# ScalarE's instructions in the program's own order, exponentials and scores in fixed turns of buffers

## The chip, the cores and the metric

The kernel runs on one core of a Trainium2 chip. The metric is the device time of one execution in microseconds, the median of three runs. A profiled execution of the same program gives the trace.

## What is computed

Input x has four images of 128 channels and 64 x 64 positions. Per image (batch):

- a group norm, a convolution that yields offsets and a mask, a deformable 3 x 3 convolution (bilinear samples gathered at shifted positions, weighted with the mask), added to x;
- each position is now a token of 128 values. A layer norm; cosines of the values plus an angle and running products of these give features for 16 heads of 8 values; attention over all 4096 tokens of the image with these features as queries, keys and values alike; an output matrix, layer norm, a small feed-forward of 512 with a relu, layer norm, added to the tokens;
- a layer norm, a router over 8 experts with softmax, the two best, and the weighted sum of their 128 x 128 products, added.

```
qkv = _qz_ring(heads + rx_theta)
scores = einsum('bhsd,bhtd->bhst', q, q) / sqrt(D)
ctx = einsum('bhst,bhtd->bhsd', softmax(scores), q)
```

Since queries and keys are the same features, the matrix of exponentials is symmetric: a tile of it, transposed, serves another pair of chunks.

## The kernel before

**Attention steps.** Tokens are cut into 8 chunks of 512, keys into 32 tiles of 128, heads into 4 groups of 4. A *run* is one (batch, group, chunk of queries); a *step* (run, t) handles key tile t of a run. There are 3700 steps, written out by a loop over n that issues the scores of step n+2 (LAG = 2) ahead of the context of step n. Per step:

- `scores` (L1250): four matmuls, one a head, into two PSUM tiles `sc` of 128 x 1024 (tag "sc", three buffers);
- two exponentials on ScalarE (L1259), from `sc` to two SBUF tiles `e` of 128 x 1024 (tag "e", six buffers);
- `context` (L1267): four matmuls (each recorded twice), which read `e` and add to the accumulator `acc`. At a run's end VectorE moves `acc` to `cu` (L1471, L1473).

In order of PE's queue: scores of step t, filler, context of step t-2, scores of step t+1.

**Tiles given away.** Four steps of most runs are in `gives`. For these `turn` (L1141) lets VectorE transpose both `e` tiles in 32 x 32 blocks into a tile `st` (three buffers), which SyncE stores to DRAM (`etd`). The next run loads them (`et`, two buffers) and uses them in `from_turned` (L1203), which saves it four steps' scores and exponentials. So an `e` tile of such a step has two readers, TensorE and VectorE.

**Work beside it.** `Beside` holds generators: `prepare` (group norm, the table of the image in DRAM, offsets, gathers by POOL at L625, weighting on VectorE at L645 to L651, transposes, convolution, features) for the next batch, `finish` (output matrix, feed-forward, experts) for chunks whose four groups are done, up to two chunks at a time, and `turned`. Each generator yields what it next needs of PE and VectorE (`need`), and the loop puts it among the steps by a plan of its own with 1.82 us a step. `beside.later(when, emit)` emits an instruction when the plan's clock reaches `when`; `beside.dve` is when the plan has VectorE done.

**Who orders.** The block of the main loop is under `tc.manual_schedule(engines={PE, DVE, SP, POOL})`: for these four engines the order of the program is kept. ScalarE isn't named, so the framework's scheduler places its instructions, and gives out the buffers of pools with more than one by its own idea of when each comes free. Besides the exponentials ScalarE runs 8 `mk` (L559, the mask's exponential), 32 `ex` (L1017, the router's softmax), and the DMA issues of the constants (`fill`, L293; those with late=True are emitted after the first table) and of six of the table's stores (L501).

The lines that the change moves:

```
        mk = temp("mk", KK, half)
        nc.scalar.activation(mk, om[:, :, 18:27], AF.Exp, scale=-1.0)
...
        nc.scalar.activation(ex, lg, AF.Exp)
```

Of the kernel before, what the change touches and what calls it, by code (L numbers as in the profile page):

```python
# [9 lines left out]
F32 = mybir.dt.float32  # L10
I32 = mybir.dt.int32
F32R = mybir.dt.float32r
AF = mybir.ActivationFunctionType
ALU = mybir.AluOpType
AX = mybir.AxisListType
PE = mybir.EngineType.PE
DVE = mybir.EngineType.DVE
SP = mybir.EngineType.SP
POOL = mybir.EngineType.Pool
PSUM = bass.MemoryType.PSUM  # L20
DRAM = bass.MemoryType.DRAM

P = 128
# [176 lines left out]
def need(pe=0.0, dve=0.0, lat=0.0, hold=False, after=0.0):  # L200

    return pe, dve, lat, hold, after


def ve(n, ops=1):

    return ops * (0.17 + n / 960.0)
# [6 lines left out]
def tr(n):  # L216

    return 0.13 + 0.115 * n
# [3 lines left out]
def kernel(  # L222
# [22 lines left out]
    nc = tc.nc  # L245
# [5 lines left out]
    big = ctx.enter_context(tc.tile_pool(name="big", bufs=1))  # L251
    work = ctx.enter_context(tc.tile_pool(name="work", bufs=2))
    dram = ctx.enter_context(tc.tile_pool(name="table", bufs=1, space=DRAM))
    ps_s = ctx.enter_context(tc.tile_pool(name="ps_s", bufs=3, space=PSUM))
    ps_a = ctx.enter_context(tc.tile_pool(name="ps_a", bufs=1, space=PSUM))
    ps_m = ctx.enter_context(tc.tile_pool(name="ps_m", bufs=1, space=PSUM))

    beside = Beside()
# [2 lines left out]

    progress = {}
    featuring = []

    summed = []


    alone = []

    def misc(name):  # L270
        if alone:
            return ps_s.tile([P, 2, 512], F32, tag="sc", name=name)[:, 0, :]
        return ps_m.tile([P, 512], F32, tag="misc", name=name)

    def by_columns(dst, lhsT, rhs, start, stop):
# [139 lines left out]
    for i in range(NFX):  # L415
        t = big.tile([P, 4, QR], F32, name=f"fx{i}")
# [91 lines left out]
    def offsets(b, xn, idx, wt, rest):  # L508


        xn3 = xn.rearrange("p (h w) -> p h w", w=WW)
        HB = NBLK // 2

        def temp(name, n, half):
            return work.tile([P, HB, n], F32, tag="p2", name=f"{name}{b}_{half}", bufs=NP2)

        def products(half, got):

            for n, k in enumerate((4, 0, 1, 2, 3, 5, 6, 7, 8)):
                for top in range(0, 8, 4):
                    last = n == KK - 1 and top == 4
                    yield need(pe=MM256, dve=ve(512) if last else 0.0, lat=0.2 if last else FREE, hold=not last)
                    if n == 0 and top == 0:
                        po = misc(f"om_ps{b}_{half}")
                        p3 = po.rearrange("p (h w) -> p h w", w=WW)
                    dy, dx = k // 3 - 1, k % 3 - 1
                    for c in range(4):
                        r0 = 32 * half + 8 * c  # L530
                        ra, rb_ = max(r0 + top, -dy), min(r0 + top + 4, HH - dy)
                        ca, cb = max(0, -dx), min(WW, WW - dx)
                        nc.tensor.matmul(  # L533
                            p3[32 * c : 32 * (c + 1), ra - r0 : rb_ - r0, ca:cb],
                            lhsT=wom_sb[:, k, :],
                            rhs=xn3[:, ra + dy : rb_ + dy, ca + dx : cb + dx],
                            start=(n == 0 and top == 0), stop=last,
                        )
            oc = work.tile([P, 512], F32, tag="p2", name=f"oc{b}_{half}", bufs=NP2)
            nc.vector.tensor_scalar(oc, po, bom_sb, None, ALU.add)  # L540
            yield need(pe=tr(4), dve=ve(432), lat=0.2)
            om = temp("om", 27, half)
            got.append(om)
            pt = misc(f"oc_ps{b}_{half}")
            for i in range(4):
                nc.tensor.transpose(
                    pt[:, P * i : P * (i + 1)], oc[:, P * i : P * (i + 1)], ident
                )
            nc.vector.tensor_copy(
                om.rearrange("p (c i) k -> p i c k", i=4),  # L550
                pt.rearrange("p (i c k) -> p i c k", c=4, k=32)[:, :, :, :27],
            )

        def rows_and_weights(half, om):
            blk = slice(HB * half, HB * (half + 1))

            yield need(dve=ve(288, 2))
            mk = temp("mk", KK, half)
            nc.scalar.activation(mk, om[:, :, 18:27], AF.Exp, scale=-1.0)  # L559
            p = om[:, :, 0:18]  # L560
            nc.vector.tensor_tensor(p, p, grid_sb[:, blk, :], ALU.add)
            nc.vector.tensor_scalar(p, p, LO, HI, ALU.max, ALU.min)
            yield need(dve=ve(288, 3))
            fl, up, ix = temp("fl", 18, half), temp("up", 18, half), temp("ix", KK, half)
            nc.vector.tensor_scalar(fl, p, ROUND, None, ALU.add)
            nc.vector.tensor_scalar(fl, fl, ROUND, None, ALU.subtract)
            nc.vector.tensor_tensor(up, fl, p, ALU.is_gt)
            yield need(dve=ve(288, 2))
            nc.vector.tensor_tensor(fl, fl, up, ALU.subtract)
            nc.vector.tensor_tensor(p, p, fl, ALU.subtract)  # L570
            yield need(dve=ve(144, 3) + 0.6)

            def of_axis(t, a):
                return t.rearrange("p j (k a) -> p j k a", a=2)[:, :, :, a]

            nc.vector.tensor_scalar(mk, mk, 1.0, None, ALU.add)
            nc.vector.reciprocal(mk, mk)
            nc.vector.tensor_scalar(
                ix, of_axis(fl, 0), float(TW), 2.0 * TW + 2.0, ALU.mult, ALU.add
            )  # L580
            nc.vector.tensor_tensor(idx[:, blk, :], ix, of_axis(fl, 1), ALU.add)
            yield need(dve=ve(288))

            nc.vector.tensor_scalar(up, p, -1.0, 1.0, ALU.mult, ALU.add)
            for dy in range(2):
                yield need(dve=ve(144, 3), lat=0.2)
                nc.vector.tensor_tensor(ix, of_axis(p if dy else up, 0), mk, ALU.mult)
                for dx in range(2):
                    nc.vector.tensor_tensor(
                        wt[:, blk, :, 2 * dx + dy], ix, of_axis(p if dx else up, 1), ALU.mult  # L590
                    )

        got = []
        yield from products(0, got)
        yield from rows_and_weights(0, got[0])
        yield from products(1, got)
        rest.append(rows_and_weights(1, got[1]))

    def deform(b, tab, idx, wt, rest):
# [320 lines left out]
    def feed_forward(b, ch, x4, a4):  # L920
# [12 lines left out]
        nc.vector.tensor_copy(zx[:, :, 0, :].bitcast(F32R), zf)  # L933
        nc.vector.tensor_tensor(zx[:, :, 2, :].bitcast(F32R), zf, zx[:, :, 0, :], ALU.subtract)
        nc.vector.tensor_copy(zx[:, :, 1::2, :], zx[:, :, 0::2, :])
        yield need(pe=tr(4), dve=ve(512), lat=0.2)
        pz = misc(f"z_ps{b}_{ch}")
        for i in range(4):
# [15 lines left out]
        for i in range(4):  # L954
            for f in range(FFN // P):
# [7 lines left out]
                    f == 0, f == FFN // P - 1,  # L963
                )
        nc.vector.tensor_tensor(a4, a4, pf.rearrange("p (i c) -> p i c", c=C), ALU.add)  # L965
        m = work.tile([P, 4], F32, tag="ln_m", name=f"m2{b}_{ch}")
        rs = work.tile([P, 4], F32, tag="ln_r", name=f"r2{b}_{ch}")
        yield from layer_norm_stats(a4, m, rs, "ln")
# [8 lines left out]
    def experts(b, ch, x4):  # L977
# [15 lines left out]
        def bcx(t):  # L993
            return t[:, :, None].to_broadcast([P, 4, NE])

        lg, ex, eq, gt = small("lg"), small("ex"), small("eq"), small("gt")
# [17 lines left out]
        )  # L1014
        nc.vector.tensor_reduce(mx, lg, AX.X, ALU.max)
        nc.vector.tensor_tensor(lg, lg, bcx(mx), ALU.subtract)
        nc.scalar.activation(ex, lg, AF.Exp)  # L1017
        for rnd in range(2):
            yield need(dve=ve(32, 7), lat=0.2)
            nc.vector.tensor_reduce(mx, ex, AX.X, ALU.max)  # L1020
# [221 lines left out]
    def scores(run, t):  # L1242
        b, g = runs[run][:2]
        ps = [
            ps_s.tile([P, 2, 512], F32, tag="sc", name=f"sc{run}_{t}_{pr}") for pr in range(2)
        ]
        kT, qT = keys[b, g, t // 4][0], queries[run]
        for i in range(4):
            h = 32 * i
            nc.tensor.matmul(  # L1250
                ps[i // 2][:, i % 2, :],
                lhsT=kT[h : h + 32, P * (t % 4) : P * (t % 4 + 1)],
                rhs=qT[h : h + 32, :],
                start=True, stop=True,
            )
        es = []
        for pr in range(2):
            e = work.tile([P, 2, 512], F32, tag="e", name=f"e{run}_{t}_{pr}", bufs=6)
            nc.scalar.activation(e, ps[pr], AF.Exp, scale=1.0 / math.sqrt(HD))  # L1259
            es.append(e)  # L1260
        return es
# [75 lines left out]
    for n, (run, t) in enumerate(steps):  # L1337
        b, g, sc = runs[run][:3]
# [53 lines left out]
    es = []  # L1392
    n = issued = begun = 0
    beside.rate = 1.0
    with tc.manual_schedule(engines={PE, DVE, SP, POOL}):
        alone.append(True)
        beside.add("prepare", prepare(0), 2)
        while (0, 0) not in prepared:
# [3 lines left out]
        while n < len(steps):  # L1402
# [10 lines left out]
            run, t = steps[n]  # L1413
            b, g, sc, ts, kind = runs[run]
# [138 lines left out]
```

## Time and profile before

| what | value |
|---|---|
| median of three runs | 7730.28 us (7711.24 to 7750.06) |
| the profiled execution | 7756.43 us, span 7754.7 us |
| granted TensorE clock, mean | 0.964 |
| PE busy / ScalarE busy | 93% / 89% |
| VectorE busy / POOL busy | 58% / 21% |
| exponentials e<-sc | 7400, mean 1066 ns |
| first exponential / last | 179.3 us / 7669.2 us |
| moved by DMA | 1730.69 MB, mean 223 GB/s |

Neighbouring exponentials overlap a little, so the mean of one is more than the time between two. A busy PE is not PE at its peak: the ends of matmuls are modelled. Before 180 us no attention step can run; until about 1000 us the first image streams in while its chunks are still prepared. Then the preparation of the second, third and fourth image lies at about 1000 to 2000, 2250 to 3700 and 4250 to 5450 us, as POOL's busy time shows. After the last exponential 85 us of finishing are left.

### The profile page before, as it was taken

To read this page: it belongs to the slowest core of one execution; us is meant where nothing else is said; L and a number is where in the kernel's file an instruction comes from. 1 tells how busy PE (TensorE), PEld (TensorE's weight loads), DVE (VectorE), ACT (ScalarE), POOL (GpSimd) and SP (SyncE) were. 2 spreads that over 40 slices of the span, in tenths; PEclk is the share of its full clock that TensorE was granted. 3 is DMA by queue.
4 is the path that set the end of the run, shared out by engine and by line. 5 is a ranking of instruction groups with operands and counts; after the bars stand their busy time and mean duration, and the time that the engine had idled before them with its cause. 6 is when DMAs were issued, how large, how long until landed. Compare 5 with 4: busy or idle time off the path is not lost.

```text
span 7754.7 us, 181999 instructions
## 1 busy us (share of the span) xinstructions
PE 7193.2 (93%) x73736; PEld 2531.8 (33%) x73736; DVE 4481.5 (58%) x8976; ACT 6874.7 (89%) x7441; POOL 1650.3 (21%) x1326
## 2 busy tenths in 40 slices
PE   3679899899999999999999989999999999999997
PEld 2222233223333333333333323333333333333333
DVE  6766356667444767766544667765444545545444
ACT  0569899789999899989999978889999999999995
POOL 5544034343001332422000333431000000000000
PEclk6889999999999999999999999999999999999998
DMA  5767477879557878888666788988665587777762
GB/s 182 219 208 226 133 233 234 276 240 288 158 161 216 256 231 269 284 257 244 199 179 186 234 259 277 300 279 260 187 181 162 151 255 237 247 239 251 241 217 75
DMA packets 922614, 1730.69 MB, mean 223 GB/s; under 512 B 169074, under 2 KB 393356, under 8 KB 871084
## 3 DMA queue, kind: packets, MB, share of 16 engines
q1 hardware_dynamic: 821918, 1412.48, 59.8%
q0 software_dynamic: 92160, 302.06, 11.9%
q8 instruction: 578, 9.47, 0.5%
q10 hardware_dynamic: 7694, 4.52, 0.2%
q14 instruction: 264, 2.16, 0.1%
HBM read 1059.11 MB, written 659.57 MB: 222 GB/s over the span
## 4 chain that ended last, share of the span: by engine, by line
PE 82%; DMA 6%; DVE 4%; issue 3%; ACT 3%; SPq 2%; POOL 0%; another core or an unknown queue 0%; ACTq 0%; DVEq 0%; POOLq 0%
PE acc L1267 40%; PE sc L1250 24%; PE acc L1203 5%; PE conv_ps L278 4%; PE e_ps L278 3%; ACT e L1259 3%; PE f_ps L278 2%; DMA et<-etd 1%; PE om_ps L533 1%; DMA sT<-smd 1%; DMA etd<-st 1%; PE ao_ps L278 0%; DVE st L1141 0%; DMA smd<-tr 0%; DVE v L645 0%
## 5 line engine op out<-in xcount | busy, mean ns | idle before, releaser
L1259 ACT ACTIVATE e<-sc 128x1024 f32<-128x1024 f32 x7400 | 6871.4, 1066 | 743.0 <-PE sc L1250 467.0
L1267 PE MATMUL acc<-e,qf 128*32 128x512 f32 x29600 | 3978.3, 607 | 36.9 <-DVE cu L1473 22.3
L1250 PE MATMUL sc<-qT,kT 32*128 32x512 f32 x14800 | 2396.8, 500 | 261.2 <-ACT e L1259 153.6
L1250 PEld LDWEIGHTS sc<-qT,kT 32*128 32x128 f32 x14800 | 958.7, 183 | 3672.2 <-ACT e L1259 3053.7
L625 POOL DMA_INDIRECT v<-tab,idx x1152 | 1447.0, 1256 | 1758.6 <-DVE tr L686 1119.4
L1141 DVE STREAM_TRANSPOSE st<-e 128x1024 f32<-128x1024 f32 x792 | 937.6, 1222 | 800.5 <-ACT e L1259 565.0
L1267 PEld LDWEIGHTS acc<-e,qf 128*32 128x32 f32 x29600 | 801.9, 110 | 609.6 <-issue 344.8
L393 POOL TENSOR_TENSOR r<-ln_t,expo 128x4 f32<-128x4 f32 x96 | 112.3, 1170 | 3142.6 <-DVE ln_t L391 3106.0
L645 DVE TENSOR_TENSOR v<-v,wt 128x1536 f32<-128x1536 f32 x384 | 666.0, 1734 | 99.0 <-DMA v<-tab,idx 78.6
L1203 PE MATMUL acc<-et,qf 128*32 128x128 f32 x12672 | 524.6, 282 | 39.5 <-DMA et<-etd 31.6
L1065 DVE TENSOR_TENSOR eo<-e_ps,gt 128x512 f32<-128x512 f32 x256 | 175.2, 686 | 542.7 <-PE e_ps L278 532.0
L1203 PEld LDWEIGHTS acc<-et,qf 128*32 128x32 f32 x12672 | 303.5, 110 | 241.6 <-issue 191.6
L650 DVE TENSOR_TENSOR v<-v 128x768 f32<-128x768 f32 x384 | 367.2, 956 | 9.7
L278 PE MATMUL conv_ps<-sT,wconv_sb 128*32 128x256 f32 x4320 | 352.4, 400 | 12.6 <-DMA sT<-smd 8.1
L1471 DVE COPY cu<-acc 128x512 f32<-128x512 f32 x128 | 88.5, 691 | 405.6 <-PE acc L1267 341.6
L686 DVE STREAM_TRANSPOSE tr<-v 128x128 f32<-128x128 f32 x1080 | 249.5, 282 | 34.5 <-DMA etd<-st 24.9
L651 DVE TENSOR_TENSOR v<-v 128x384 f32<-128x384 f32 x384 | 215.7, 562 | 13.3
L393 POOL TENSOR_TENSOR rstd<-lt_t,expo 128x4 f32<-128x4 f32 x32 | 59.4, 1857 | 525.6 <-DVE lt_t L391 494.9
L278 PE MATMUL f_ps<-w_sb,h 128*32 128x128 f32 x4096 | 166.6, 282 | 1.1 <-issue 1.0
L950 DVE TENSOR_SCALAR h<-h_ps,b_sb 128x512 f32<-128x512 f32 x128 | 95.0, 744 | 102.4 <-PE h_ps L948 90.3
L823 POOL COPY fx<-rn 128x512 f32<-128x512 f32 x32 | 26.8, 836 | 540.3 <-DVE rn L822 361.8
L965 DVE TENSOR_TENSOR a<-a,f_ps 128x512 f32<-128x512 f32 x32 | 22.0, 687 | 201.8 <-PE f_ps L278 201.8
(224 smaller groups left out, 3146.9 us busy)
## 6 DMA issues: line engine op xcount, KB each, us to landing
etd<-st SPq DMA_DIRECT2D x1584, 256.0 KB
et<-etd SPq DMA_DIRECT2D x396, 1024.0 KB
kT<-kTd SPq DMA_DIRECT2D x400, 256.0 KB
smd<-tr SPq DMA_DIRECT2D x360, 192.0 KB
sT<-smd SPq DMA_DIRECT2D x360, 192.0 KB
qf<-fqd SPq DMA_DIRECT2D x400, 144.0 KB
qT<-qTd SPq DMA_DIRECT2D x166, 256.0 KB
atd<-cu SPq DMA_DIRECT2D x128, 256.0 KB
```

The source lines that it names most:

```text
L278: nc.tensor.matmul(dst[c : c + 32], lhsT=lhsT[:, c : c + 32], rhs=rhs, start=start, stop=stop)
L625: nc.gpsimd.indirect_dma_start(out=v[:, k, :], out_offset=None, in_=tab, in_offset=bass.IndirectOffsetOnAxis(ap=idx[:, j, kk : kk + 1], ax ...
L645: nc.vector.tensor_tensor(v4, v4, w12[:, :, None].to_broadcast([P, 12, C]), ALU.mult)
L650: nc.vector.tensor_tensor(v[:, :, : 2 * C], v[:, :, : 2 * C], v[:, :, 2 * C :], ALU.add)
L651: nc.vector.tensor_tensor(v[:, :, :C], v[:, :, :C], v[:, :, C : 2 * C], ALU.add)
L686: nc.vector.transpose(out=tr9[:, k, :, j % 4, :], in_=v[:, k, :C].rearrange("p (c i) -> p c i", i=32),)
L1065: nc.vector.tensor_tensor(ws[hf], pe.rearrange("p (e c) -> p e c", c=C), gt[:, i, 4 * hf : 4 * (hf + 1), None].to_broadcast([P, 4, C]), AL ...
L1141: nc.vector.transpose(out=st[:, :, 2 * pr : 2 * pr + 2, :].rearrange("p o h (q j) -> p o (h q) j", j=32), in_=es[pr].rearrange("p h (q o i ...
L1203: nc.tensor.matmul(acc[32 * h : 32 * (h + 1), P * kt : P * (kt + 1)], lhsT=qf[:, t, QW * h : QW * h + 32], rhs=e[:, :, h, 32 * t : 32 * (t ...
L1250: nc.tensor.matmul(ps[i // 2][:, i % 2, :], lhsT=kT[h : h + 32, P * (t % 4) : P * (t % 4 + 1)], rhs=qT[h : h + 32, :], start=True, stop=True,)
L1259: nc.scalar.activation(e, ps[pr], AF.Exp, scale=1.0 / math.sqrt(HD))
L1267: nc.tensor.matmul(acc[32 * h : 32 * (h + 1), :], lhsT=qf[:, t % 4, QW * h : QW * h + 32], rhs=es[h // 2][:, h % 2, :], start=(t == ts[0]) ...
```

## The change

- `ACT` joins the engines of the manual schedule: ScalarE's instructions stand in the order in which the program emits them.
- A helper `in_turn` gives out the tiles of "sc" (three) and "e" (six) in a fixed turn, each place a tag of its own with one buffer.
- `mk` and `ex` are emitted by `beside.later` when the plan has VectorE done with their input; the `need` ahead of `mk` gains a latency of 0.5.
- In `feed_forward` a list `feeding` lets only one chunk be between its first transposes and the last sum of its feed-forward part.

```diff
-    ps_s = ctx.enter_context(tc.tile_pool(name="ps_s", bufs=3, space=PSUM))
+    ps_s = ctx.enter_context(tc.tile_pool(name="ps_s", bufs=1, space=PSUM))
...
+    feeding = []
...
+    taken = {}
+
+    def in_turn(pool, tag, n, shape, name, dt=F32):
+        k = taken[tag] = taken.get(tag, -1) + 1
+        return pool.tile(shape, dt, tag=f"{tag}{k % n}", name=name, bufs=1)
 
     def misc(name):
         if alone:
-            return ps_s.tile([P, 2, 512], F32, tag="sc", name=name)[:, 0, :]
+            return in_turn(ps_s, "sc", 3, [P, 2, 512], name)[:, 0, :]
...
-            yield need(dve=ve(288, 2))
+            yield need(dve=ve(288, 2), lat=0.5)
             mk = temp("mk", KK, half)
-            nc.scalar.activation(mk, om[:, :, 18:27], AF.Exp, scale=-1.0)
+            beside.later(
+                beside.dve,
+                lambda: nc.scalar.activation(mk, om[:, :, 18:27], AF.Exp, scale=-1.0),
+            )
...
         nc.vector.tensor_copy(zx[:, :, 1::2, :], zx[:, :, 0::2, :])
+
+        while feeding:
+            yield need(lat=0.5)
+        feeding.append(True)
         yield need(pe=tr(4), dve=ve(512), lat=0.2)
...
         nc.vector.tensor_tensor(a4, a4, pf.rearrange("p (i c) -> p i c", c=C), ALU.add)
+        feeding.clear()
...
-        nc.scalar.activation(ex, lg, AF.Exp)
+        beside.later(beside.dve, lambda: nc.scalar.activation(ex, lg, AF.Exp))
...
         ps = [
-            ps_s.tile([P, 2, 512], F32, tag="sc", name=f"sc{run}_{t}_{pr}") for pr in range(2)
+            in_turn(ps_s, "sc", 3, [P, 2, 512], f"sc{run}_{t}_{pr}") for pr in range(2)
         ]
...
-            e = work.tile([P, 2, 512], F32, tag="e", name=f"e{run}_{t}_{pr}", bufs=6)
+            e = in_turn(work, "e", 6, [P, 2, 512], f"e{run}_{t}_{pr}")
             nc.scalar.activation(e, ps[pr], AF.Exp, scale=1.0 / math.sqrt(HD))
...
-    with tc.manual_schedule(engines={PE, DVE, SP, POOL}):
+    with tc.manual_schedule(engines={PE, DVE, SP, POOL, ACT}):
```

More of the change, by code (lines that the diff above doesn't have):

```diff
@@ L19 @@
 POOL = mybir.EngineType.Pool
+ACT = mybir.EngineType.Activation
 PSUM = bass.MemoryType.PSUM
```

## The prediction

> **What bounds the kernel now.** I read the page's engine totals first, then the table of busy time by stage, then ScalarE's waits, and last the order of instructions in one stretch.
>
> ```profile
> PE 7193.2 (93%) x73736; PEld 2531.8 (33%) x73736; DVE 4481.5 (58%) x8976; ACT 6874.7 (89%) x7441; POOL 1650.3 (21%) x1326
> ```
>
> Two engines are near full, so the totals don't say which one sets the pace. The stages do (columns: length, then busy time and instructions of PE, PEld, DVE, ACT, POOL, the granted clock, the DMA share, GB/s):
>
> ```profile
> 1000.00:2000.00 1000.00, 931.53 (x8432) 304.72 (x8432) 612.14 (x1034) 883.88 (x951) 369.96 (x293) 0.97 0.81 252
> 2000.00:2250.00 250.00, 249.54 (x2618) 88.53 (x2610) 136.53 (x341) 249.59 (x274) 8.64 (x9) 1.00 0.58 169
> 2250.00:3700.00 1450.00, 1372.01 (x14433) 485.54 (x14433) 945.38 (x1814) 1313.69 (x1420) 396.19 (x318) 0.98 0.78 243
> 3700.00:4250.00 550.00, 548.92 (x6071) 198.02 (x6067) 266.61 (x598) 548.90 (x597) 14.76 (x15) 1.00 0.65 189
> 4250.00:5450.00 1200.00, 1110.15 (x11113) 382.93 (x11113) 819.71 (x1503) 1042.46 (x1123) 391.19 (x311) 0.97 0.85 266
> 5450.00:7650.00 2200.00, 2191.72 (x24619) 795.77 (x24611) 1050.38 (x2444) 2189.40 (x2388) 53.35 (x52) 1.00 0.69 212
> ```
>
> In the quiet stages (2000, 3700 and 5450 us on) ScalarE is busy over 99% of the time: 274 instructions in 250 us, one exponential in 0.91 us, two to a step, 1.83 us a step. There ScalarE is the bound and nothing can be had. In the three stages in which the next batch is prepared (POOL busy, DMA share about 0.8) it is idle for 116 + 136 + 158 = 410 us. Its own waits between 1000 and 5500 us say on what:
>
> ```profile
> ACT e L1259 <- PE sc L1250: 165.8, 147, 8.7
> ACT e L1259 <- PE acc L1267: 152.4, 137, 2.7
> ...
> ACT e L1259 <- DVE st L1141: 8.2, 4, 5.8
> ```
>
> The second row is the odd one. An exponential reads scores (sc); why should it wait for a context matmul (acc)? Only because that matmul still reads the buffer e that the exponential is to overwrite. The stretch around 2655 us shows what this costs, first on ScalarE, then on TensorE:
>
> ```profile
> 2649.38 5.61 ACT L1259 ACTIVATE e<-sc 128x1024 f32<-128x1024 f32 x6 [1.19 <-PE sc L1250]
> 2656.21 1.94 ACT L1259 ACTIVATE e<-sc 128x1024 f32<-128x1024 f32 x2 [1.23 <-PE acc L1267]
> 2659.32 1.94 ACT L1259 ACTIVATE e<-sc 128x1024 f32<-128x1024 f32 x2 [1.17 <-PE acc L1267]
> ```
>
> ```profile
> 2652.32 0.50 PE L1250 MATMUL sc<-qT,kT 32*128 32x512 f32 x4
> 2652.75 0.64 PE L1203 MATMUL acc<-et,qf 128*32 128x128 f32 x16
> 2653.21 1.04 PE L1267 MATMUL acc<-e,qf 128*32 128x512 f32 x8
> 2654.18 0.51 PE L1250 MATMUL sc<-qT,kT 32*128 32x512 f32 x4
> ...
> 2656.05 0.49 PE L1250 MATMUL sc<-qT,kT 32*128 32x512 f32 x2
> 2657.29 0.51 PE L1250 MATMUL sc<-qT,kT 32*128 32x512 f32 x2 [0.74 <-ACT e L1259]
> 2657.72 0.64 PE L1203 MATMUL acc<-et,qf 128*32 128x128 f32 x16
> 2658.18 1.04 PE L1267 MATMUL acc<-e,qf 128*32 128x512 f32 x8
> 2659.16 0.50 PE L1250 MATMUL sc<-qT,kT 32*128 32x512 f32 x2
> ```
>
> A step with 16 filler matmuls takes 2654.18 - 2652.32 = 1.86 us while the buffers are free, and the same work takes 2659.16 - 2656.05 = 3.11 us in the stalled form. It is a loop between two engines: exp(t) waits for context(t-2), which stands behind scores(t) on TensorE; the second half of scores(t+1) waits for exp(t)'s first half, since there are three score buffers; context(t-1) stands behind that. In steps of this kind the two engines work by turns. VectorE is no cause here: it idles 7.63 us up to 2666.56, itself waiting for an exponential.
>
> **What the Trainium skill says.** "Perfetto Trace Analysis", section "Optimization Strategy": the same gap repeating on the engine that should be saturated can mean that the next tile finds no buffer. The trace agrees: 137 gaps of 1.1 us. "ScalarE: Activation LUTs", section "What ACT_TABLE_LOAD costs", gives an activation 186 ns plus 0.833 ns an element, neighbours overlapping by 93 ns: for 1024 columns an estimate of 1.04 us long and 0.95 us apart. The trace has a median of 1.04 us and 0.91 us apart, so the exponentials run at their floor and only gaps can be saved.
>
> **The change part by part.** All sums are made against the profiled execution (7756.43 us, span 7754.7), which is 26 us above the median of 7730.28; I move the difference over to the median.
>
> 1. *Buffers of e in turn.* In the built program before, the six e buffers are handed out by a planner's idea of what is free. Of 7394 reuses, 6974 are six exponentials apart, 267 are four apart, 29 five, 124 eight to sixteen. Two buffers are taken to be held by the 32x32 transposes (L1141, run for the runs that give tiles away), and the exponentials go round in the other four. Four apart is two steps, and that is the loop above. Matching records with the program, the four-apart ones carry 134 gaps with 157 us. In the built program after, every reuse is six apart, and context(t-3) stands ahead of scores(t) on TensorE, so this wait can't bind. Two prices agree: the wait row, 152 us; and step lengths from 1000 us on, by filler matmuls in the step: stalled 2.76 us against 1.88 (under 8; 29 steps), 3.16 against 1.93 (8 to 15; 78), 3.26 against 1.98 (16 to 23; 21), 3.64 against 3.20 (24 on; 5): 26 + 96 + 27 + 2 = 151 us. The second already contains that TensorE has its filler to do. I take **-152**.
>
> 2. *What the ring waits for instead.* In the program after, the exponential three steps behind a transposed one waits for the two transposes. There are 396 such pairs, 2.4 us of VectorE each. In the trace of before, the second transpose ends later than the start of the exponential six on in 11 pairs, by 37 us in all. If exponentials kept a pace of 1.83 us a step, so that the buffer were wanted 5.49 us after the start of the one transposed, it would be 21 pairs and 82 us. The latest of them waits for an st buffer whose stores are on their way (VectorE idle 12.84 us up to 1721.47, <-DMA etd<-st). While an exponential waits for that, all exponentials queue behind it, then scores, then context. Between 37 and 82 I take 60, less the 8.2 us that ScalarE waits for st already: **+52**.
>
> 3. *The score buffers in turn.* They were three apart before and are three apart after: **0**, unless one of the misc() tiles at the ends shifts.
>
> 4. *ScalarE's order.* The 7400 exponentials keep their order. The 40 short ones (mk, ex) stand two to eight exponentials later against their neighbours. Before, ScalarE had no gap ahead of them but at the ends (0.4 us in all otherwise); later means safer, unless VectorE runs late. VectorE's instructions that read mk and ex come 2 to 7 us later, covered by its 30 to 40% idle time. **0**; 40 times 1 us is the upper end if VectorE is behind.
>
> 5. *Start.* On ScalarE's DMA queue seven weight loads and two of the vectors' (issued 21.70 to 26.03 us) now stand behind the six tab stores, which can go at 21.2, 24.6 and 28.2 when VectorE's copies end. At 1.3 us an issue the stores end near 30.8 instead of 34.0; the loads follow, 4.3 + 12.0 us (34.44 to 46.40), and mk's table load begins near 47.1 instead of 46.40. The first gather (50.22) follows idx, which stands behind mk on VectorE: +0.7, bounds -4 and +4. On SyncE's and POOL's queues nothing changes before the second batch's preparation; after that the same instructions stand a few places earlier or later.
>
> 6. *feeding.* Two finishing chunks may no longer be inside their feed-forward parts together. That is filler on TensorE and VectorE, with no end to meet but the last: after the last context matmul the program before has 226 matmuls, the one after 194; 32 expert matmuls, two of the 3.04 us rounds on VectorE (7675.61 to 7678.65), leave the tail ahead of the last reciprocal: **-5**.
>
> 7. *Less time for the same transfers.* Preparation is tied to steps, so 150 us less over 3650 us raise a DMA share of 0.78 to 0.85 by 4%. Stores of st and sT loads land later: not shown, bounded by 0 and 40 (the 77 us for which transposes wait on etd<-st, grown by half), I take **+10**.
>
> Sum: -152 + 52 + 0 + 0 + 1 - 5 + 10 = -94, taken as -90. 7730 - 90 = **7640 us**.
>
> **The rivals.**
> - *More goes.* 42 further waits after 2350 us, 34 us in all, end with a context matmul though the profile names a score long done; if these are the same loop, and the late pairs stay at 37: 7730 - 152 - 34 + 29 - 5 + 5 = 7573. Against it: their reuses are six apart.
> - *The gain is eaten (no change).* If stall-free steps make VectorE 1.5 us later at every transposition, the late time at full pace is 138 us by the same count: 7730 - 152 + 130 + 5 = 7713.
> - *Slower: VectorE becomes the bound of the ring.* Before, a late transpose cost two buffers of six; now it stops all exponentials. The preparing stages have VectorE at 61 to 68%, the plan lets it run 3.2 us behind, and stalled steps had given it time. Price: at a lag of 2 us the late time is 182 us, at 2.5 us 241 us, at 3 us 330. Break-even is near 1.7 us, slower by over 0.5% from 2.1. At 2.5: 7730 - 152 + 233 + 5 = 7816. Against it: the median pair has 2.5 to 3 us to spare, and a stall lets VectorE catch up.
> - *The order alone does nothing:* true of parts 3 and 4, and counted so.
>
> **How the numbers follow.** Forecast case 0.60, more goes 0.13, eaten 0.12, slower 0.15. A measurement here can tell about 0.5% (39 us) from no change, so faster is below 7691, slower above 7769. The forecast case with part 2 at its ends and part 7 at 40 spans 7600 to 7690. The range reaches down to the larger gain, 7565, and up over the eaten case into the slower one, 7755. Faster 0.73, same 0.12, slower 0.15.
>
> **What would show it.** Right: the row of e waiting for acc falls from 152 us to a few; ScalarE's idle time in the three preparing stages falls from 410 us to near 310; a new row e <- st of some 60 us appears; quiet stages keep 0.91 us an exponential. Wrong: e <- st at 150 us or more, or e <- sc growing by what acc lost (TensorE's filler was the bound), or a first gather later than 54 us.

## The result, and the profile after

| | median | range | runs |
|---|---|---|---|
| before | 7725.96 us | 7711.24 to 7750.06 | 6 |
| after | 7673.61 us | 7669.46 to 7688.59 | 6 |

The ratio is 0.9936, interval 0.9922 to 0.9949: 52 us less, where the forecast was 90. The two profiled executions are 68 us apart (7756.43 and 7688.59 us), since the one of before is further above its median than the one of after. Chips differ more than the two kernels do: on three others the kernel before took 7587, 7718 and 7584 us, so times are compared by their ratio to the kernel before on the same chip.

ScalarE's waits between 1000 and 5500 us, after (us in total, times, longest):

```profile
ACT e L1277 <- PE sc L1268: 249.0, 163, 20.4
ACT e L1277 <- remote: 49.6, 19, 7.4
ACT e L1277 <- DVE st L1159: 29.1, 9, 7.9
...
ACT e L1277 <- PE acc L1285: 2.8, 2, 1.5
```

The wait for context matmuls is gone: 152.4 us became 2.8. The wait for transposes grew to 29.1 us (8.2 before). The first line is the surprise: exponentials wait 249.0 us for scores, 165.8 before. The forecast had named a growth of this line by what acc lost as a sign of being wrong; it came by 83 of 150 us. TensorE's own waits in the same stretch say what it was late for, after:

```profile
PE sc L1268 <- ACT e L1277: 73.3, 57, 6.4
PE acc L1221 <- DMA et<-etd: 46.3, 8, 9.3
...
PE conv_ps L288 <- DMA sT<-smd: 31.2, 8, 13.1
PE ao_ps L288 <- DVE aT L914: 20.3, 2, 19.0
```

and before:

```profile
PE sc L1250 <- ACT e L1259: 132.9, 172, 3.0
PE acc L1203 <- DMA et<-etd: 31.6, 13, 7.2
...
PE conv_ps L278 <- DMA sT<-smd: 6.4, 4, 3.1
```

TensorE waits less for exponentials (133 to 73 us) and more for filler inputs: turned tiles (et), the convolution's samples (sT), the attention output (aT), 38 us before and 98 us after. Filler stands in TensorE's queue ahead of the next scores, so ScalarE runs dry behind it. The longest of these waits shows it, on TensorE and then on ScalarE:

```profile
5106.89 1.08 PE L288 MATMUL ao_ps<-wcomb_sb,aT 128*32 128x128 f32 x16 [18.98 <-DVE aT L914]
5107.75 1.93 PE L1285 MATMUL acc<-e,qf 128*32 128x512 f32 x8
5109.61 0.80 PE L1268 MATMUL sc<-qT,kT 32*128 32x512 f32 x4
```

```profile
5110.50 1.94 ACT L1277 ACTIVATE e<-sc 128x1024 f32<-128x1024 f32 x2 [20.39 <-PE sc L1268]
```

How the 60 us more of such waits became 83 us on ScalarE was not worked out. The stages, after (columns as in the table of before):

```profile
1000.00:2000.00 1000.00, 933.95 (x8512) 303.81 (x8504) 627.45 (x1072) 894.62 (x966) 380.61 (x294) 0.96 0.81 252
...
2250.00:3700.00 1450.00, 1359.48 (x14274) 478.64 (x14274) 927.26 (x1774) 1305.03 (x1413) 389.38 (x319) 0.97 0.80 245
...
4250.00:5450.00 1200.00, 1136.79 (x11892) 399.40 (x11888) 818.64 (x1558) 1103.01 (x1196) 363.40 (x292) 0.98 0.84 260
```

ScalarE's idle time in the three preparing stages is 105 + 145 + 97 = 347 us, 410 before and near 310 in the forecast. (The windows lie at fixed times; in them ScalarE of after runs 81 more instructions.)

### The profile page after: what moved, and what is told of

Its sections match the earlier page's. It is cut to its first block, busy times and chain, and to the rows that moved or that the text cites. A ratio compares the mean times of both kernels' runs of the same rounds, so it can differ in the third digit from the quotient of the medians.

```text
span 7685.8 us, 181979 instructions
## 1 busy us (share of the span) xinstructions
PE 7132.5 (93%) x73736; PEld 2511.6 (33%) x73736; DVE 4476.9 (58%) x8976; ACT 6864.9 (89%) x7441; POOL 1651.8 (21%) x1326
## 4 chain that ended last, share of the span: by engine, by line
PE 80%; DMA 6%; DVE 5%; issue 4%; SPq 2%; ACT 1%; POOL 1%; another core or an unknown queue 0%; POOLq 0%; ACTq 0%; DVEq 0%
PE acc L1285 38%; PE sc L1268 23%; PE acc L1221 5%; PE conv_ps L288 4%; PE e_ps L288 3%; PE f_ps L288 2%; ACT e L1277 1%; DMA sT<-smd 1%; DMA et<-etd 1%; DMA etd<-st 1%; DMA rdd<-rd 1%; DVE v L658 1%; POOL v L638 1%; DVE st L1159 1%; PE om_ps L543 1%
## 5 line engine op out<-in xcount | busy, mean ns | idle before, releaser
L1268 PE MATMUL sc<-qT,kT 32*128 32x512 f32 x14800 | 2344.5, 500 | 197.7 <-ACT e L1277 91.4
L1268 PEld LDWEIGHTS sc<-qT,kT 32*128 32x128 f32 x14800 | 942.7, 183 | 3569.2 <-ACT e L1277 3032.1
L288 PE MATMUL f_ps<-w_sb,h 128*32 128x128 f32 x4096 | 165.8, 280 | 0.6 <-issue 0.6
```

The lines of the kernel that those rows point to most:

```text
L288: nc.tensor.matmul(dst[c : c + 32], lhsT=lhsT[:, c : c + 32], rhs=rhs, start=start, stop=stop)
L1268: nc.tensor.matmul(ps[i // 2][:, i % 2, :], lhsT=kT[h : h + 32, P * (t % 4) : P * (t % 4 + 1)], rhs=qT[h : h + 32, :], start=True, stop=True,)
```

## The experiments

The theory after the result has two halves. First: the turn of buffers removed the loop between exp(t) and context(t-2), as forecast. Second: the loop's stalls had also given transfers time. The plan counts latencies in steps of 1.82 us; when steps really last 1.83 us and not 3.1, an input planned to be there has not landed. Rivals: the fixed order of ScalarE made the gain; the feeding gate made the new waits; TensorE's filler is simply too long for a step; planned latencies would have helped as much without the turn. The expectations below were written with this theory. The runs bear out its first half and not its second: the late inputs are there before the turn is (the first and the third experiment).

### The order without the turns

The changed kernel with the pools' own buffers again:

```diff
-            e = in_turn(work, "e", 6, [P, 2, 512], f"e{run}_{t}_{pr}")
+            e = work.tile([P, 2, 512], F32, tag="e", name=f"e{run}_{t}_{pr}", bufs=6)
```

and the same for sc, with three.

> The changed kernel, but e and sc come from pools with six and three buffers again; ScalarE's fixed order, the later emission of mk and ex and the feeding gate stay. In the built program 191 of the reuses of an e buffer are four exponentials apart (267 before, none after). Theory (the buffers are what counts, the order is worth nothing by itself): exponentials wait for context matmuls (e <- acc) for about 155 us x 191/267 = 110 us, and some third of that reaches the end as it did in the change: about 7710 us. Rival (the order is what counts): e <- acc is small all the same, or it is there and the time is within 10 us of the changed kernel's 7674.

Measured: ratio 1.0030 (1.0018 to 1.0042), 7615 us beside 7587. Waits from 1000 to 5500 us, of ScalarE and then of TensorE:

```profile
ACT e L1277 <- PE sc L1268: 188.6, 53, 18.9
ACT e L1277 <- PE acc L1285: 109.1, 99, 2.6
ACT e L1277 <- DVE st L1159: 14.7, 5, 8.0
```

```profile
PE acc L1221 <- DMA et<-etd: 68.6, 14, 11.3
PE conv_ps L288 <- DMA sT<-smd: 50.4, 10, 10.6
PE ao_ps L288 <- DVE aT L914: 19.2, 2, 17.8
```

The wait for acc is 109.1 us, as scaled from the 191 reuses. The time of 7710 us was for another chip; as a ratio it would have been 0.998, and 1.003 is worse than that. So the order is not what gains, and since the reuses four apart are back, so is the loop.

Nothing but the buffers separates this kernel from the changed one: in the two traces the 8976 instructions of VectorE, the 7441 of ScalarE and the 4657 transfers of SyncE's queue stand in the same sequence (tiles by name, buffer numbers left out). And the late inputs are here already, 138.2 us of waits for et, sT and aT, though most of the loop's stalls are left.

### The turn without the order

The kernel before with e from `in_turn` alone.

> The kernel before, with only the e tiles in turn of six; ScalarE is left to the scheduler. In the built program the exponentials then no longer stand in the order of their steps: in ScalarE's order reuses are from two to ten apart. Theory (turn and order are one change: without the fixed order the scheduler lets later exponentials pass one whose buffer it takes to be held): e waits for acc or sc as much as before or more, 7700 to 7780 us. Rival (the turn alone is enough): e <- acc under 20 us and 7660 to 7690 us.

Measured: ratio 1.0098 (1.0082 to 1.0114), 7664 us, above the forecast's upper end (7780 us would have been 1.007).

```profile
ACT e L1265 <- PE sc L1256: 330.1, 234, 9.7
ACT e L1265 <- DVE st L1147: 14.3, 6, 4.0
```

The wait for acc has no line left, but exponentials wait 330 us for scores, and a new line of TensorE, context matmuls waiting for exponentials, has 49.8 us (28 times). With a fixed turn and a free order the scheduler puts later exponentials ahead, and the context of the one passed waits. In this kernel the turn gains only together with the order.

### The feeding gate

The kernel before with the gate alone.

> The kernel before with the feeding gate alone. Theory (filler moved within slack): 7726 us within 12 us; e <- acc stays at about 155 us. Rival (the gate delays finishing chunks, and the waits of the output matrix for a<-rdd that grew from 7 to 32 us come from it): 7740 us or more, with PE's ao_ps waiting over 20 us.

Measured: ratio 0.9995 (0.9986 to 1.0003), 7587 us. The gate alone does nothing to the time. Waits from 1000 to 5500 us, of ScalarE and then of TensorE:

```profile
ACT e L1265 <- PE acc L1273: 155.8, 141, 2.4
ACT e L1265 <- PE sc L1256: 112.5, 44, 9.4
```

```profile
PE acc L1209 <- DMA et<-etd: 47.0, 17, 6.3
PE conv_ps L279 <- DMA sT<-smd: 19.6, 5, 8.4
```

TensorE waits 66.6 us for et and sT and not at all for aT. Beside the order without the turns, measured on the same chip, this tells where the late inputs come from. What that kernel has more is ScalarE's fixed order, the later mk and ex, and the latency of 0.5 ahead of mk. With these the waits for et, sT and aT go from 66.6 to 138.2 us, ScalarE's wait for scores from 112.5 to 188.6, and the time from 7587 to 7615 us, while the wait for acc falls by 47 and that for st by 3. The rows (-47 + 76 - 3) give +26 us, the medians +28.

Of the three, the 0.5 is the only edit that the plan sees, and it moved the plan: from about 955 us on VectorE's instructions stand in another sequence than here. The wait for mk and ex themselves is small (VectorE waits 22.9 us for them in the same stretch, 2.7 here). So the likely cause is that filler was moved to places where the old latencies are too short. No run has the 0.5 alone.

### Longer planned latencies

The changed kernel, with filler planned to use its inputs later:

```diff
-            yield need(lat=2.5)
+            yield need(lat=5.0)
...
             get(0)
-            yield need(lat=6.0)
+            yield need(lat=9.0)
             get(1)
-            yield need(lat=4.0)
+            yield need(lat=10.0)
...
-        yield need(lat=4.0)
+        yield need(lat=6.0)
...
-        yield need(lat=6.0)
+        yield need(lat=9.0)
         a4 = temp2(f"a4_{b}_{ch}")
...
+        yield need(lat=12.0)
         yield from attention_out(b, ch, r, aT, a4)
```

> The changed kernel with longer planned latencies for transfers: convolved 2.5, 6, 4 become 5, 9, 10; finish 4 and 6 become 6 and 9, and 12 us are added after the issue of a<-rdd. Theory (what the freed buffers gave was partly lost since steps run faster than before while transfers do not, so that filler's inputs are not there: PE waited for et, sT and aT 38 us before and 98 us after between 1000 and 5500 us): PE's waits for sT and aT fall from 51 us to under 15, e <- sc from 249 to about 200, the time to about 7635 us. Rival (TensorE's filler itself is too long for a step, transfers don't matter): 7665 to 7685 us with e <- sc at 240 or more. Second rival (the chunks get behind and are forced at the end of a batch): over 7690 us.

Measured: ratio 0.9840 (0.9824 to 0.9856), 7463 us beside 7587; the forecast of 7635 us would have been 0.988. To set it against the changed kernel on one chip, both ran on another:

> The changed kernel, as the control of this call. Everybody: e <- acc under 5 us. If chips on which the kernel before takes near 7590 us show fewer waits of ScalarE that no theory here names (e <- sc of about 1 us with the score long done, e <- remote), the ratio there may differ from the 0.9937 seen where it takes near 7720: 0.985 to 0.995.

> lat_more beside the changed kernel on one chip. Theory (late inputs of filler took back half of the gain): faster than the changed kernel by 0.5 to 1.0% of the kernel before, that is by 40 to 75 us, since lat_conv alone had 0.46%; PE's waits for sT and aT under 15 us. Rival (most of the 0.984 of the first look came from that chip): within 0.3% of the changed kernel.

| one chip, before 7584.29 us | median | ratio | interval |
|---|---|---|---|
| changed kernel | 7526.85 us | 0.9923 | 0.9910 to 0.9936 |
| with longer latencies | 7456.11 us | 0.9833 | 0.9819 to 0.9847 |

71 us less than the changed kernel, 0.9% of the kernel before. TensorE's waits from 1000 to 5500 us in the changed kernel on this chip:

```profile
PE acc L1221 <- DMA et<-etd: 65.1, 16, 10.1
PE conv_ps L288 <- DMA sT<-smd: 63.1, 11, 13.2
PE sc L1268 <- ACT e L1277: 24.1, 12, 5.4
PE ao_ps L288 <- DVE aT L914: 19.1, 2, 17.8
```

and with longer latencies:

```profile
PE acc L1222 <- DMA et<-etd: 77.3, 20, 8.7
PE sc L1269 <- ACT e L1278: 32.7, 8, 9.5
PE conv_ps L288 <- DMA sT<-smd: 1.9, 1, 1.9
```

The waits for sT and aT fall from 82.2 to 1.9 us, and ScalarE's wait for scores from 201.6 to 108.7. Nothing of the filler was made shorter, so the rival of too much filler falls for this part. et was not touched, and stays.

The changed kernel here also shows what the turn adds to the order alone, on two chips alike in speed (7587 and 7584 us for the kernel before): the waits for et, sT and aT are 147.3 us where they were 138.2, ScalarE's wait for scores 201.6 where it was 188.6, for st 32.2 where it was 14.7, and the wait for acc, 109.1 there, has no line. The rows (-109 + 13 + 17) give -79 us, the ratios (1.0030 to 0.9923) 1.07%, about 81 us. So of the late inputs' growth from 66.6 us (gate alone) to 147.3, 72 us came without the turn and 9 with it.

### The same latencies without the turn and the order

> The kernel before with the feeding gate (which did nothing by itself: ratio 0.9995) and the longer planned latencies of lat_more; buffers and ScalarE's order stay with the scheduler, 259 reuses of e four apart. Theory (the turn gives 150 us of ScalarE's idle time, of which late transfers took half in the change; latencies alone help before only by the 38 us that PE waited for transfers there): e <- acc stays near 155 us, 0.990 to 0.997. Rival (the latencies did it all in lat_more, the turn is worth little): 0.984 to 0.988.

Measured: ratio 1.0012 (1.0004 to 1.0020), no gain at all. ScalarE's waits from 1000 to 5500 us:

```profile
ACT e L1266 <- PE acc L1274: 143.9, 127, 2.7
ACT e L1266 <- PE sc L1257: 124.5, 120, 12.3
```

The loop kept its 143.9 us. The latencies had little to remove: TensorE waits 1.1 us for sT, 6.4 in the kernel before, and in this stretch for aT in neither. The forecast of 0.990 to 0.997 had counted on 38 us, but 31.6 of them are waits for et, which these latencies don't touch (34.3 us here). The rival is wrong by more. The latencies are worth 0.9% in the changed kernel and nothing here; since turn, order and the 0.5 are all missing here, this run doesn't say which of them makes the difference.

Read the other way, it shows what the change is worth when these inputs are in time on both sides: 1.0012 without it, 0.9833 to 0.9840 with it, by estimate 1.7 to 1.8% (on different chips), or some 130 us.

### Which latencies, and the changed kernel beside it

> The changed kernel once more, beside the kernels of this call on one chip. All theories: 0.9936 of the kernel before within 0.003; e waits for acc under 5 us; PE's waits for et, sT and aT between 1000 and 5500 us near 98 us, e <- sc near 250 us or less.

> The changed kernel with the longer latencies in convolved alone (2.5, 6, 4 become 5, 9, 10), those of finish as in the change. Theory (each late input costs what PE waits for it; sT 31 us and aT 20 us between 1000 and 5500 us, aT 12 us more outside): PE's wait for sT goes, that for aT stays, 0.988. Rival (the gain of lat_more came from finish): 0.991 or more.

Measured on one chip (before 7717.99 us): changed kernel 0.9937 (0.9924 to 0.9951), latencies of `convolved` alone 0.9891 (0.9875 to 0.9906). With those of `convolved` alone TensorE has no line for sT left in this stretch (30.1 us in the changed kernel beside it), that for aT has 12.1 us (18.9), and ScalarE's e <- sc is 168.5 us instead of 235.7. The 0.46% are 36 us (41 by the medians), near the 30 us of waiting for sT, and the forecast of 0.988 lies in the interval.

### The turned tiles asked for earlier

The kernel with longer latencies (lat_more) with two edits:

```diff
-        fetched[run, kt] = e, beside.now + 16.0
+        fetched[run, kt] = e, beside.now + 21.0
...
-                if run + 1 in takes and at == len(ts) - 5:
+                if run + 1 in takes and at == len(ts) - 8:
```

> lat_more, and the turned tiles asked for eight steps ahead of a run's end instead of five and planned to land after 21 us instead of 16. Theory: the largest wait of PE on a transfer left in lat_more (et<-etd, 82 us) falls under 30 us and the ratio goes from 0.984 to about 0.976. Rival (with two et buffers the second pair is asked for only when the first is used, so an earlier start doesn't bring it): et<-etd at 60 us or more and a ratio within 0.003 of 0.984. Second rival (the giving run's stores are not landed yet eight steps ahead, and SyncE's queue waits for them): slower than lat_more.

> Turned tiles asked for earlier and planned later. Theory: in its first run et<-etd fell to 12 us between 1000 and 5500 us, but e <- st rose to 57, so it ends within 0.3% of lat_more on the same chip. Rival: faster than lat_more by 0.5% or more.

Measured: 0.9882 (0.9865 to 0.9899) on the chip with before at 7717.99 us, where 0.976 was forecast, and 0.9855 (0.9838 to 0.9871) beside lat_more's 0.9833. So it is no better than lat_more, by the medians 17 us slower, with intervals that overlap. ScalarE's waits from 1000 to 5500 us in the second run:

```profile
ACT e L1278 <- DVE st L1160: 98.6, 24, 16.5
ACT e L1278 <- PE sc L1269: 53.5, 37, 9.4
```

The wait for et fell from 77.3 to 20.3 us, and e <- sc with it, but the transposes came later: e <- st grew from 38.1 to 98.6 us. SyncE's queue shows a likely cause. It waits 622.2 us for a free et tile at the fetch (L1204), 392.7 in lat_more, and the stores of st are issued on the same queue behind that. That link was not tried by itself.

### Four buffers

The changed kernel with a turn of four, so that every exponential is in the loop; one execution.

```diff
-            e = in_turn(work, "e", 6, [P, 2, 512], f"e{run}_{t}_{pr}")
+            e = in_turn(work, "e", 4, [P, 2, 512], f"e{run}_{t}_{pr}")
```

> The changed kernel with a turn of four e buffers instead of six, so that every exponential stands in the loop with the context matmul two steps earlier. Theory (price of the loop): a step without filler 2.66 us and with 8 to 15 filler matmuls about 3.1 instead of 1.83; 3700 steps at 0.8 to 1.25 us more give 10600 to 12000 us, e <- acc over 2500 us, and ScalarE about 60% busy. Rival (the waits at acc only stood where TensorE was late anyway): under 9000 us.

Measured: 12824.71 us. ScalarE's waits over the whole run, then TensorE's order in a stretch of it:

```profile
ACT e L1277 <- PE acc L1285: 5304.9, 3681, 6.2
```

```profile
6000.40 0.50 PE L1268 MATMUL sc<-qT,kT 32*128 32x512 f32 x2 [0.74 <-ACT e L1277]
6000.83 0.64 PE L288 MATMUL e_ps<-ew_sb,u_7T 128*32 128x256 f32 x8
6001.29 1.04 PE L1285 MATMUL acc<-e,qf 128*32 128x512 f32 x8
6002.26 0.50 PE L1268 MATMUL sc<-qT,kT 32*128 32x512 f32 x2
6003.50 0.50 PE L1268 MATMUL sc<-qT,kT 32*128 32x512 f32 x2 [0.74 <-ACT e L1277]
```

A step with eight filler matmuls lasts 6003.50 - 6000.40 = 3.10 us, the price taken from the kernel before, with the same 0.74 us of TensorE's idling. ScalarE waits for a context matmul 3681 times in 3700 steps. The loop is confirmed. The total is above the forecast of 10600 to 12000 us: over the whole run a context matmul took 742 ns on average, 607 in the kernel before, at a granted TensorE clock of 0.81. That this is the reason was not tested.

## Why the prediction was right, and where its sum was off

The direction, the range and the mechanism of the turn held; the gain was 52 us for a forecast of 90. What the forecast had at nothing is that the change moves other work to places where its inputs are late. By its steps, on the profiled pair:

1. *e in turn, -152.* The row fell from 152.4 to 2.8 us. The order without the turns keeps 109.1 us of it and gains nothing, though its instructions stand in the same sequence as in the changed kernel; four buffers give the loop to all steps and reproduce the 3.10 us. The mechanism is shown.
2. *Late transposes, +52.* Over-sized: the row grew by 21 us (8.2 to 29.1, nine waits). The reasons named were the right kind. Five of the late pairs follow a transpose at the head of VectorE's queue that waits for a store, etd<-st, and the longest wait a VectorE that stood still for aT:

```profile
3073.52 0.69 DVE L914 TENSOR_TENSOR aT<-aT,a 128x512 f32<-128x512 f32 x1 [19.00 <-DMA a<-rdd]
3074.13 1.75 DVE L658 TENSOR_TENSOR v<-v,wt 128x1536 f32<-128x1536 f32 x1
3075.80 2.36 DVE L1159 STREAM_TRANSPOSE st<-e 128x1024 f32<-128x1024 f32 x2
```

   The exponential after it started at 3077.13, 7.92 us late. The rival in which VectorE becomes the bound did not come: its price began at 182 us of late time, and 29 us came.

3. *Scores in turn, 0.* Not tried by itself; nothing seen speaks against it.
4. *ScalarE's order, 0.* **Here, with a remark in part 5, the working went wrong.** It looked at what mk and ex could cost directly, and that was little. Part 5 says of SyncE's and POOL's queues that from the second image's preparation on their instructions "stand a few places earlier or later"; VectorE's and TensorE's do so too, and no term has a price for it. With the order, the later mk and ex and the moved plan, but without the turn, TensorE's waits for late inputs grow from 66.6 to 138.2 us, ScalarE's wait for scores by 76 us, and the time by 28 us. The forecast also did not see that without the order the turn is a loss (1.0098).
5. *Start, +1.* The first exponential starts at 179.6 us, 179.3 before; the first gather 2.1 us later, within the bounds.
6. *feeding, -5.* From the last exponential pair to the end 80.5 us, 86.4 before. The gate alone: nothing.
7. *Less time for the same transfers, +10.* DMA share stayed at 0.80 to 0.84. The part of the late inputs that came with the turn itself is small, as forecast: 9 us on TensorE, 13 in ScalarE's wait for scores.

On the profiled pair the rows give -150 + 21 + 83 - 6 = -52 where the forecast had -94. The pair itself is 68 us apart, so the rows miss it by 16 us, and that their sum equals the difference of the medians is chance. Two errors partly cancel: late transposes were priced 31 us too high, the wait for scores behind late inputs 73 us too low (+10 for 83). That the forecast came within 38 us of the measured gain is in part luck.

The rival "more goes" is refuted by the time (7573 us). Many of the waits that it counted, with a score long done, go with the chip: the changed kernel has 163 waits for scores in this profile and 57 on a faster chip. The rival "eaten" (7713 us) was nearer in kind, since part of the gain was eaten, but by late filler and not by late transposes.

The best version measured is the one with longer planned latencies: 0.9833 of the kernel before, 0.9% below the changed kernel.

## What to carry to other kernels

When an engine that should be saturated waits for a *reader* of the buffer that it is to overwrite, look at how far apart reuses are in the built program: two buffers thought to be busy turned a ring of six into one of four and made two engines work by turns. When a change moves a plan of other work, even a little, look anew at whether each input lands in time: latencies that were long enough in the old places were not in the new ones, and a few longer constants gave more (71 us) than the whole change had (52 to 57). And take a change apart before explaining what it lost: the stalls that went and the late inputs that came appeared in the same profile, but a run with everything except the turn had the late inputs too. In this kernel a fixed turn of buffers needs a fixed order of the engine that fills them; the turn alone was 1.0% slower than neither, the order with its moved plan alone 0.3%.

## What the runs showed of the hardware that was not expected

With four buffers TensorE waits 0.65 us a step for an exponential (2404.2 us in 3682 waits, none over 1.0 us), and its granted clock is 0.81 (0.964 in the kernel before); no run here separates the idling from other causes.

The kernel before takes 7584 to 7587 us on two chips and 7718 to 7726 us elsewhere. Where it is slower ScalarE has waits that it lacks where it is faster: from 1000 to 5500 us, e <- remote (released by no instruction that the profile shows) 49.3 us, and e <- sc 165.8 us in 147 waits, where the kernel with the gate alone, within 0.1% of the kernel before, has 112.5 us in 44 and none on remote. Over the whole run all six profiles from elsewhere have 37 to 65 us of waits on remote, the eight from the two faster chips none. What delays them was not settled.
